# Moving the comparison of later choices into the loop over experts, and the choices of all four batches behind the end of L0

## The chip, the cores and the metric

The kernel runs on one core of a Trainium2 chip. Its time is the device time of one execution in microseconds (us), taken as the median of several runs. The engines are TensorE (PE for its matmuls, PEld for loading their stationary operand), VectorE (DVE), ScalarE (ACT), GpSimd (POOL) and SyncE (SP, which here only issues DMAs). Each works through its own instructions in their written order and waits for the others by semaphores.

## The reference

The program is two layers, L0 and L1, each an attention and a feed-forward part, over 4 batches of 256 tokens with 256 features, in float32. L0 is an attention with rounded weights and inputs, then a mixture of 32 experts; L1 is a cross attention and a gated feed-forward net. What matters here is L0's mixture of experts:

```python
router_probs = softmax(x @ gate_weight.T)
router_top_value, router_indices = top_k(router_probs, 8)
routing_weights = router_top_value / clip(sum(router_top_value), 1e-12)
prim, sec = router_indices[:, :4], router_indices[:, 4:]
sim_cand = sim[sec[:, :, None], prim[:, None, :]]
best_sim, best_i = max(sim_cand, -1), argmax(sim_cand, -1)
new_sec = where(best_sim < 0.5, sec, prim[best_i])
combine = sum(one_hot(concat(prim, new_sec)) * routing_weights)
y = sum over experts e of combine[:, e] * (silu(x @ wg[e].T) * (x @ wu[e].T)) @ wd[e].T
```

(x is the layer-normed input; the result is added to the residual stream. Lines are shortened.) Each token has eight chosen experts. The four later choices are compared with the four first ones by a table of similarities, and a later choice that is similar enough hands its weight to a first one. What is left with a weight of its own among the later choices is computed by a rarely needed second pass.

L1's attention lets a token see only the keys whose number lies in a window that ends at the token's segment id; the mask of that window is called `bad` in the kernel.

## The kernel before, in words

**L0's attention** runs as 16 units: four groups of heads (c) times four batches (b), unit u = 4c + b. Each unit is cut into small steps (projection, norms, scores, softmax, gather, rounding, output), and the order of all steps of all units is written out: `PLACE` gives each kind of step a place, `SHIFT` moves it by unit, and line 977 sorts them into one list, `line`. Each engine issues its steps in that order. A hundred places are meant as about one us. Step Y (line 887) adds a unit's output to the residual stream `xs`; the last, of unit 15, is the end of L0, and `done` is its place.

**The route of a batch** (class `Route`) is put into the same list when the last group of heads (units 12 to 15) is reached. Its steps: statistics and mean of the rows (DVE, lines 299 and 302), an epsilon, the power that makes the reciprocal deviation (POOL, line 308), the norm (DVE, 311), the turn by transposes (PE, 320) and its copy (ACT, 323), the router's logits (PE, 329), maximum, exponential and softmax (337 to 347), the choice of eight (351, 352), its one-hot form (357), the members of each expert (364), ranks within an expert by matmuls (PE, 374 to 381), places (389, 392) and goals (397 to 402). A step's place is that of the batch's own Y plus 100 times the step's number plus `WAIT` of the batch.

**The set-up of L1** folds weights of L1's attention (lines 1053 to 1129, mostly PE and ACT) and is placed from `done` on, spaced by `SPREAD`. All of this is under a hand-written order, up to line 1146.

**From line 1147 on a planner places the instructions**: it takes them in written order as priority, but may put one that is ready into a hole of its engine earlier. First come the 32 scatters (line 406: POOL issues a DMA that writes 128 rows of a batch to the rows `rows_in` of their experts in DRAM), eight a batch, then the slots (416, 417). Then comes the comparison: four transposes of the one-hots of later choices into a bank (1180), their copy (1184), a matmul with the similarities for each of eight row tiles (1189), a product (1191) and a sum (1197) on DVE, then a score of small DVE steps that end in the weights `wf` (1221) and the flag `isleft` (1227, 1229), and the mask `bad` (1239 to 1243).

**The loop over experts** (1308 to 1321) has 34 turns. In a turn it issues the load of an expert's 256 rows `xe` (SP, 1282), their transposes (PE, 1290) and the copy `xeT` (DVE, 1292), the gate and up products of the expert before (PE 1273, ACT 1275, DVE 1276), and the down product of the one before that (PE 1299, ACT 1304) with its write to `rows_out` (SP, 1305). The weights of two experts are loaded at a time. After the loop the flag is read (1323) and, if it is set, the second pass runs. Then L1's attention gathers rows back with POOL's DMAs (1355), weights them by `wf` (1358), and goes on to the rest.

Tiles live in pools. Those of the set-up lie in `set1`, as do those of the comparison; `set1` is closed before the loop's pool `experts` is opened, so that its tiles take the same memory.

Of the kernel before, what the change touches and what calls it, by code (L numbers as in the profile page):

```python
# [7 lines left out]
F32 = mybir.dt.float32  # L8
# [4 lines left out]
I32 = mybir.dt.int32  # L13
AF = mybir.ActivationFunctionType
ALU = mybir.AluOpType
AX = mybir.AxisListType
PSUM, DRAM = bass.MemoryType.PSUM, bass.MemoryType.DRAM

P = 128
B, S, H = 4, 256, 256  # L20
SC = 64
# [33 lines left out]

WAIT = [50, 52, 21, 0]
SPREAD = 135


PLACE = {
# [46 lines left out]
def build(tc, ctx, t, out):  # L109
# [7 lines left out]
    def bank(name):  # L117
        return psum.tile([P, 512], F32, tag="bank", name=name)
# [143 lines left out]
    class Route:  # L262
# [24 lines left out]

        def get(self, tag, shape, dtype=F32):
            if tag not in self.tile:
                self.tile[tag] = small.tile(shape, dtype, tag="rt_" + tag, bufs=2, name=f"rt_{tag}_{self.name}")  # L290
            return self.tile[tag]

        def bank(self, name):
# [125 lines left out]
        def parts(self):  # L419

            d = [
                (0.2, self.stats, 0), (0.6, self.stats, 1), (1.0, self.mean, 0), (1.2, self.mean, 1), (1.5, self.eps),
                (2.0, self.power), (3.2, self.norm, 0), (3.7, self.norm, 1), (4.8, self.turn), (6.0, self.turned),
                (7.5, self.logits), (9.0, self.largest), (9.8, self.exponential), (10.4, self.softmax),
                (11.2, self.choose, 0), (11.6, self.choose, 1), (12.2, self.choices), (13.2, self.members),
                (14.6, self.ranks), (15.8, self.places), (16.8, self.goals),
            ]
            return d

    routes = [Route(b) for b in range(B)]  # L430
    with ExitStack() as l0:
# [532 lines left out]
                d["Y"] = (0, self.residual)  # L964
                return d

        line = []
        for u in range(4 * B):
            for name, (kind, *call) in Unit(u).parts().items():
                place = PLACE[name] + SHIFT[0][u] + (SHIFT[kind][u] if kind else 0)  # L970
                line.append((place, u, name, call))
                if name == "Y":
                    done = place
            if u >= 3 * B:
                for m, (behind, *call) in enumerate(routes[u - 3 * B].parts()):
                    line.append((done + 100 * (behind + WAIT[u - 3 * B]), u, f"route{m:02d}", call))
        line.sort(key=lambda x: x[:3])

        later = [x for x in line if x[0] > done]
# [52 lines left out]
    with moe as l0:  # L1032
# [123 lines left out]

        one = set1.enter_context(tc.tile_pool(name="moe1", bufs=1, reuse_waits="tile"))
        work = set1.enter_context(tc.tile_pool(name="moe", bufs=1, reuse_waits="tile"))  # L1160
        offd = one.tile([P, P], F32, name="offd")
        nc.vector.tensor_scalar(offd[:], ident[:], -1.0, 1.0, ALU.mult, ALU.add)
        nc.vector.tensor_tensor(simb[:], simb[:], offd[:], ALU.mult)
        nc.vector.tensor_tensor(simb[:], simb[:], ident[:], ALU.add)
        ones = one.tile([P, P], F32, name="ones")
        nc.gpsimd.memset(ones[:], 1.0)

        wt = route.tile([P, NT, TOPK], F32, name="wt")
        m8 = one.tile([P, NT], F32, name="m8")
        nc.vector.tensor_reduce(m8[:], tv[:], AX.X, ALU.add)  # L1170
        nc.vector.tensor_scalar(m8[:], m8[:], 1e-12, None, ALU.max)
        nc.vector.reciprocal(m8[:], m8[:])
        nc.vector.tensor_tensor(wt[:], tv[:], m8[:].unsqueeze(2).to_broadcast([P, NT, TOPK]), ALU.mult)

        cand = one.tile([P, NT, NSEL, NSEL], F32, name="cand")
        for m in range(2):
            pt = bank(f"ps_oh_{m}")
            for i in range(4):
                n = 4 * m + i
                nc.tensor.transpose(  # L1180
                    pt[:, i * P : (i + 1) * P], routes[n // 2].oh()[:, n % 2, NSEL:, :].rearrange("p k e -> p (k e)"), ident[:]
                )
            ohT = work.tile([P, 512], F32, tag="ohT", name=f"ohT_{m}")
            nc.scalar.copy(ohT[:], pt[:])
            rows = bank(f"ps_sim_{m}")
            for i in range(4):
                n = 4 * m + i
                cut = slice(i * P, (i + 1) * P)
                nc.tensor.matmul(rows[:, cut], ohT[:, cut], simb[:], start=True, stop=True)
                pd = work.tile([P, NSEL, NSEL, NE], F32, tag="pd", name=f"pd_{n}")  # L1190
                nc.vector.tensor_tensor(
                    pd[:],
                    rows[:, cut].rearrange("p (j e) -> p j e", j=NSEL).unsqueeze(2).to_broadcast([P, NSEL, NSEL, NE]),
                    routes[n // 2].oh()[:, n % 2, :NSEL, :].unsqueeze(1).to_broadcast([P, NSEL, NSEL, NE]),
                    ALU.mult,
                )
                nc.vector.tensor_reduce(cand[:, n], pd[:], AX.X, ALU.add)

        cv = cand[:].rearrange("p n j i -> p (n j) i")
        NJ = NT * NSEL  # L1200
        best = one.tile([P, NJ], F32, name="best")
        nc.vector.tensor_reduce(best[:], cv, AX.X, ALU.max)
        eq = one.tile([P, NJ, NSEL], F32, name="eq")
        nc.vector.tensor_tensor(eq[:], cv, best[:].unsqueeze(2).to_broadcast([P, NJ, NSEL]), ALU.is_equal)
        left = one.tile([P, NJ], F32, name="left")
        nc.vector.tensor_scalar(left[:], eq[:, :, 0], -1.0, 1.0, ALU.mult, ALU.add)
        for i in range(1, NSEL):
            nc.vector.tensor_tensor(eq[:, :, i], eq[:, :, i], left[:], ALU.mult)
            if i < NSEL - 1:
                nc.vector.tensor_tensor(left[:], left[:], eq[:, :, i], ALU.subtract)  # L1210
        wu = one.tile([P, NJ], F32, name="wu")
        wuv = wu[:].rearrange("p (n j) -> p n j", n=NT)
        nc.vector.tensor_scalar(wu[:], best[:], THRESHOLD, None, ALU.is_ge)
        nc.vector.tensor_tensor(wuv, wuv, wt[:, :, NSEL:], ALU.mult)
        nc.vector.tensor_tensor(wt[:, :, NSEL:], wt[:, :, NSEL:], wuv, ALU.subtract)
        nc.vector.tensor_tensor(eq[:], eq[:], wu[:].unsqueeze(2).to_broadcast([P, NJ, NSEL]), ALU.mult)
        gain = one.tile([P, NT, NSEL], F32, name="gain")
        nc.vector.tensor_reduce(gain[:], eq[:].rearrange("p (n j) i -> p n i j", n=NT), AX.X, ALU.add)
        nc.vector.tensor_tensor(wt[:, :, :NSEL], wt[:, :, :NSEL], gain[:], ALU.add)

        nc.vector.tensor_tensor(wf[:], wt[:, :, :NSEL], room[:], ALU.mult)
        nc.vector.tensor_tensor(wt[:, :, :NSEL], wt[:, :, :NSEL], wf[:], ALU.subtract)
        some = one.tile([P, 1], F32, name="some")
        nc.vector.tensor_reduce(some[:], wt[:].rearrange("p n k -> p (n k)"), AX.X, ALU.max)
        nc.vector.tensor_scalar(some[:], some[:], 0.0, None, ALU.is_gt)
        ps = bank("ps_left")
        nc.tensor.matmul(ps[:, :1], ones[:], some[:], start=True, stop=True)
        isleft = route.tile([P, 1], I32, name="isleft")
        nc.vector.tensor_scalar(isleft[:], ps[:, :1], 0.0, None, ALU.is_gt)


        seg = one.tile([P, NT], F32, name="seg")
        nc.vector.tensor_copy(seg[:], segi[:])
        seglo = one.tile([P, NT], F32, name="seglo")
        nc.vector.tensor_scalar(seglo[:], seg[:], -float(LOOKBACK), None, ALU.add)
        kid = one.tile([P, SC], F32, name="kid")
        nc.gpsimd.iota(kid[:], [[1, SC]], base=0, channel_multiplier=0, allow_small_or_imprecise_dtypes=True)
        for n in range(NT):
            nc.vector.tensor_scalar(bad[:, n, :], kid[:], seg[:, n : n + 1], None, ALU.is_le)
            nc.vector.scalar_tensor_tensor(  # L1240
                bad[:, n, :], kid[:], seglo[:, n : n + 1], bad[:, n, :], ALU.is_ge, ALU.mult
            )
        nc.vector.tensor_scalar(bad[:], bad[:], -1.0, -NEG, ALU.add, ALU.mult)

        set1.close()
        ew = {}
        work = l0.enter_context(tc.tile_pool(name="experts", bufs=3, reuse_waits="tile"))
# [1 line left out]
        def expert_weights(g):  # L1249
# [11 lines left out]
            )  # L1261
            return w


        def products(w, j, x, width, name):

# [41 lines left out]
        for step in range(NE + 2):  # L1308
            if step < NE:
                if step % EW == 0:  # L1310
                    ew[step // EW] = expert_weights(step // EW)
                xe[step] = taken(step)
            if step == 6:
                nc.sync.dma_start(w_dq[:], t["W_dq"].rearrange("(k p) n -> p k n", p=P))
                nc.sync.dma_start(w_qr[:], t["W_qr"])
                nc.sync.dma_start(w_qrs[:], t["W_qrs"])
# [293 lines left out]
```

## Time and profile before

| what | us |
|---|---|
| median of 3 runs | 924.29 (923.53 to 925.32) |
| the profiled execution, its own time | 923.63 |
| its span, first to last instruction | 921.8 |
| last Y (end of L0) begins | 519.38 |
| scatters of batch 0 on POOL | 498.5 to 509.4 |
| scatters of batch 1 | 524.2 to 534.2 |
| scatters of batches 2 and 3 | 538.1 to 558.1 |
| first transposes of expert rows | 581.5 |
| first gather back | 690.3 |

Over the span PE is busy 84%, DVE 67%, ACT 46% and POOL 44%, and the mean granted clock of PE is 0.93 of full speed.

How to read a line of the engines in order of time: start in us, length in us, engine, line of the kernel, operation, output<-inputs, sizes, count; in brackets how long the engine sat idle before and what released it. A matmul of float32 shows as two instructions. "SPq" is SP issuing a DMA, where the length includes standing in its queue; several may be merged in one line. Places where L0 ends and the experts begin lie between 480 and 600 us.

### The profile page before, as it was taken

What the parts mean: (1) busy time and instruction counts of PE and PEld (TensorE: products, weight loads), DVE (VectorE), ACT (ScalarE), POOL (GpSimd) and SP (SyncE); (2) the same over time, 40 slices, a digit from 0 to 9 for tenths busy, and PEclk for the clock granted to TensorE, in tenths of its full rate; (3) what the DMA queues carried; (4) which work ended last, traced back from release to release, by engine and by line L of the source; (5) the groups of instructions that cost most, each with busy time, mean ns of one, the idle gap of its engine ahead of it and who ended that gap; (6) DMA issues with size and microseconds to landing.
All of it is one profiled execution on the core that took longest, in us unless ns stands there. A gap on an engine that the chain in (4) does not pass through costs nothing. (4 is left out here: it accounts for less than half of the span.)

```text
span 921.8 us, 12377 instructions
## 1 busy us (share of the span) xinstructions
PE 773.5 (84%) x4026; PEld 589.9 (64%) x4026; DVE 620.2 (67%) x1649; ACT 420.5 (46%) x1111; POOL 405.1 (44%) x442
## 2 busy tenths in 40 slices
PE   1687998999989989989896897799951778897996
PEld 1466776787767778777774663688840566675454
DVE  3989989788998788887886755433314786665211
ACT  1567785588766758567582243133320111212210
POOL 2556655456564754657556561000006773341001
PEclk8679999999999999999998897799985797999999
DMA  4201101002010100830009522488834210000001
GB/s 152 69 1 47 35 1 58 1 1 81 1 58 1 47 24 1 287 125 1 2 1 220 163 102 74 129 272 270 275 111 137 65 41 1 1 0 7 0 9 37
DMA packets 46101, 66.97 MB, mean 73 GB/s; under 512 B 6672, under 2 KB 28880, under 8 KB 45968
## 3 DMA queue, kind: packets, MB, share of 16 engines
q1 hardware_dynamic: 41872, 56.17, 19.8%
q0 software_dynamic: 3072, 8.39, 2.8%
q10 hardware_dynamic: 1088, 1.57, 0.5%
q8 instruction: 33, 0.54, 0.3%
q14 instruction: 36, 0.29, 0.1%
HBM read 44.10 MB, written 22.02 MB: 72 GB/s over the span
## 5 line engine op out<-in xcount | busy, mean ns | idle before, releaser
L578 POOL TENSOR_TENSOR hn_rs<-hn_var,mhalf 128x6 f32<-128x6 f32 (+1 forms) x64 | 76.5, 1211 | 90.0 <-DVE hn_var L571 82.0
L1355 POOL DMA_INDIRECT y<-rows_out,slot x32 | 32.2, 1005 | 146.9 <-issue 136.0
L560 POOL TENSOR_TENSOR fp_q<-cat,cc 128x1024 fp32r<-128x1024 bf16 x32 | 69.0, 2156 | 51.1 <-DVE cat L558 32.9
L782 POOL TENSOR_SCALAR p<-p,rc 128x256 f32<-128x256 f32 x128 | 65.6, 528 | 26.6 <-DVE rc L777 20.3
L727 ACT ACTIVATE qn_x<-ps_px,hn_nb,hn_rs 128x128 f32<-128x128 f32 x128 | 48.2, 457 | 50.0 <-DVE hn_nb L582 45.6
L880 PE MATMUL ps_y<-wp,fp_q 128*128 128x256 f32 x512 | 69.2, 293 | 2.0 <-issue 2.0
L880 PEld LDWEIGHTS ps_y<-wp,fp_q 128*128 128x128 f32 x512 | 64.4, 195 | 7.1 <-issue 6.8
L771 ACT ACTIVATE p<-ps_s,mx 128x256 f32<-128x256 f32 x128 | 62.2, 511 | 12.0 <-DVE mx L764 11.6
L800 PE MATMUL ps_o<-pT,v 128*128 128x512 f32 x128 | 64.5, 628 | 3.1 <-ACT pT L793 2.8
L753 PE MATMUL ps_s<-kT,qT 128*128 128x256 f32 x256 | 65.8, 386 | 0.6 <-ACT qn_q L727 0.5
L1273 PE MATMUL ps_g<-xeT,wgu 128*96 128x256 f32 x256 | 62.3, 387 | 0.0
L727 ACT ACTIVATE qn_q<-ps_pq,hn_nb,hn_rs 128x128 f32<-128x128 f32 x128 | 53.0, 481 | 1.7 <-DVE hn_nb L582 1.7
L753 PEld LDWEIGHTS ps_s<-kT,qT 128*128 128x128 f32 x256 | 45.4, 192 | 7.3 <-issue 1.8
L764 DVE TENSOR_REDUCE mx<-ps_s 128x2 f32<-128x512 f32 x64 | 43.3, 681 | 7.3 <-PE ps_s L753 6.9
L1273 PEld LDWEIGHTS ps_g<-xeT,wgu 128*96 128x96 f32 x256 | 40.9, 167 | 11.1 <-DVE xeT L1292 0.3
L582 DVE SCALAR_TENSOR_TENSOR hn_nb<-hn_ms,hn_rs 128x6 f32<-128x6 f32 (+1 forms) x64 | 34.0, 532 | 19.1 <-POOL hn_rs L578 16.6
L808 ACT ACTIVATE cat<-ps_o,r_sm 128x256 bf16<-128x256 f32 x64 | 27.5, 491 | 37.1 <-PE ps_o L800 37.1
L1276 DVE TENSOR_TENSOR hT<-hT,ps_g 96x256 f32<-96x256 f32 x32 | 13.3, 417 | 45.3 <-ACT hT L1275 45.3
L793 ACT COPY pT<-ps_pt 128x512 f32<-128x512 f32 x64 | 38.2, 630 | 10.0 <-PE ps_pt L789 10.0
L1275 ACT ACTIVATE hT<-ps_g 96x256 f32<-96x256 f32 x32 | 12.2, 380 | 63.5 <-PE ps_g L1273 63.5
L703 PE MATMUL ps_px<-wqx,xq 128*128 128x512 f32 x128 | 40.1, 436 | 0.6 <-DVE wqx L533 0.3
L789 PE MATMUL ps_pt<-ident,p 128*128 128x128 f32 x256 | 37.6, 274 | 3.2 <-POOL p L782 3.1
(290 smaller groups left out, 2041.6 us busy)
## 6 DMA issues: line engine op xcount, KB each, us to landing
rows_in<-zeros SPq DMA_DIRECT2D x4, 2048.0 KB, 16.1
xe<-rows_in SPq DMA_DIRECT2D x32, 256.0 KB, 3.9
rows_out<-ye SPq DMA_DIRECT2D x32, 256.0 KB, 3.5
wgu<-in_wgu SPq DMA_DIRECT2D x16, 384.0 KB, 4.0
wp<-in_wproj SPq DMA_DIRECT2D x8, 512.0 KB, 3.9
wd<-in_wd SPq DMA_DIRECT2D x16, 192.0 KB, 3.2
w_W_o<-in_W_o SPq DMA_DIRECT2D x1, 2048.0 KB, 9.8
wq<-in_wq SPq DMA_DIRECT2D x3, 512.0 KB, 4.3
```

What stands on the lines that cost most here:

```text
L560: nc.gpsimd.tensor_tensor(dst, y, cb, ALU.subtract)
L578: nc.gpsimd.tensor_tensor(rs[:, a:z], var[:, a:z], mhalf[:, a:z], ALU.pow)
L703: nc.tensor.matmul(dst, xq[self.b][:, j, k, tok], wt[:, k, half, :], start=(k == 0 and half == 0), stop=(k == KC - 1 and half == 1))
L727: nc.scalar.activation(qn[:, cut], src[:, cut], AF.Identity, bias=nb[:, at + h : at + h + 1], scale=rs[:, at + h : at + h + 1])
L753: nc.tensor.matmul(sc[:, h * S : (h + 1) * S], qT[:, 2 * g + h, i * P : (i + 1) * P], kT[:, g, :], start=True, stop=True)
L764: nc.vector.tensor_reduce(self.four("mx", g)[:, 2 * i : 2 * i + 2], self.bank(f"s_{g}{i}")[:].rearrange("p (h s) -> p h s", h=2), AX.X, AL ...
L771: nc.scalar.activation(self.p(g, i)[:, h, :], self.bank(f"s_{g}{i}")[:, h * S : (h + 1) * S], AF.Exp, bias=self.four("mx", g)[:, at], accu ...
L782: nc.gpsimd.tensor_scalar(p[:, h, :], p[:, h, :], self.four("rc", g)[:, at], 1.0, ALU.mult, ALU.mult)
L793: nc.scalar.copy(pT[:, :, :, i * P : (i + 1) * P], self.bank(f"pt_{g}{i}")[:].rearrange("p (m h s) -> p m h s", m=2, h=2))
L800: nc.tensor.matmul(o[:], v[:, m, g * D : (g + 1) * D], pT[:, m].rearrange("p h s -> p (h s)"), start=(m == 0), stop=(m == 1))
L880: nc.tensor.matmul(y[:, i * H : (i + 1) * H], q[:, h, i * P : (i + 1) * P], wp[self.c][:, 4 * j + h, m, :], start=(fresh and h == 0 and m ...
L1273: nc.tensor.matmul(dst, w["gu"][:, j, m, k, :], x[:, k], start=(k == 0), stop=(k == KC - 1))
```

## The change

It has three parts.

1. The routes of all four batches are placed by one clock: by `done`, the place of the last Y, instead of each by its own batch's Y. `WAIT` becomes -7, 0, 3, 6 (times 100 places) and a new `LAG` of 1.6 is added behind the power, and half of it again before the softmax. The small tiles of a route have four buffers instead of two.
2. `SPREAD` goes from 135 to 120, so that the set-up's steps are placed closer together.
3. The comparison, the flag and the mask become a function, `what_is_left`, with the same instructions in the same order. It is called in the loop over experts, at step 8, behind that step's `taken`; its tiles come from the loop's pool `experts` (one buffer each), and `set1` is closed before.

```diff
-WAIT = [50, 52, 21, 0]
-SPREAD = 135
+WAIT = [-7, 0, 3, 6]
+LAG = [1.6, 1.6, 1.6, 1.6]
+SPREAD = 120
...
-                self.tile[tag] = small.tile(shape, dtype, tag="rt_" + tag, bufs=2, name=f"rt_{tag}_{self.name}")
+                self.tile[tag] = small.tile(shape, dtype, tag="rt_" + tag, bufs=B, name=f"rt_{tag}_{self.name}")
...
-                (2.0, self.power), (3.2, self.norm, 0), (3.7, self.norm, 1), (4.8, self.turn), (6.0, self.turned),
-                (7.5, self.logits), (9.0, self.largest), (9.8, self.exponential), (10.4, self.softmax),
-                (11.2, self.choose, 0), (11.6, self.choose, 1), (12.2, self.choices), (13.2, self.members),
-                (14.6, self.ranks), (15.8, self.places), (16.8, self.goals),
+                (1.6, self.power), (1.6 + LAG[self.b], self.norm, 0), (2.1 + LAG[self.b], self.norm, 1), (3.2 + LAG[self.b], self.turn), (4.4 + LAG[self.b], self.turned),
+                (5.9 + LAG[self.b], self.logits), (7.4 + LAG[self.b], self.largest), (8.2 + LAG[self.b], self.exponential),
+                (8.8 + LAG[self.b] * 1.5, self.softmax), (9.6 + LAG[self.b] * 1.5, self.choose, 0), (10.0 + LAG[self.b] * 1.5, self.choose, 1),
+                (10.6 + LAG[self.b] * 1.5, self.choices), (11.6 + LAG[self.b] * 1.5, self.members),
+                (13.0 + LAG[self.b] * 1.5, self.ranks), (14.2 + LAG[self.b] * 1.5, self.places), (15.2 + LAG[self.b] * 1.5, self.goals),
...
-        line = []
+        line, chosen = [], []
...
-                    line.append((done + 100 * (behind + WAIT[u - 3 * B]), u, f"route{m:02d}", call))
+                    chosen.append((100 * (behind + WAIT[u - 3 * B]), u, f"route{m:02d}", call))
+        line += [(done + behind, *x) for behind, *x in chosen]
...
-        one = set1.enter_context(tc.tile_pool(name="moe1", bufs=1, reuse_waits="tile"))
-        work = set1.enter_context(tc.tile_pool(name="moe", bufs=1, reuse_waits="tile"))
-        offd = one.tile([P, P], F32, name="offd")
...
         set1.close()
         ew = {}
         work = l0.enter_context(tc.tile_pool(name="experts", bufs=3, reuse_waits="tile"))
...
+        def what_is_left():
+
+            offd = work.tile([P, P], F32, name="offd", bufs=1)
+            nc.vector.tensor_scalar(offd[:], ident[:], -1.0, 1.0, ALU.mult, ALU.add)
...
+            for m in range(2):
+                pt = bank(f"ps_oh_{m}")
...
+                ohT = work.tile([P, 512], F32, tag="ohT", bufs=1, name=f"ohT_{m}")
+                nc.scalar.copy(ohT[:], pt[:])
...
+                    pd = work.tile([P, NSEL, NSEL, NE], F32, tag="pd", bufs=1, name=f"pd_{n}")
...
+            nc.vector.tensor_scalar(bad[:], bad[:], -1.0, -NEG, ALU.add, ALU.mult)
+            return wt, isleft
...
                 xe[step] = taken(step)
+            if step == 8:
+                wt, isleft = what_is_left()
             if step == 6:
```

More of the change, by code (lines that the diff above doesn't have):

```diff
@@ L1152, in build @@
             r.slots()
-        one = set1.enter_context(tc.tile_pool(name="moe1", bufs=1, reuse_waits="tile"))
-        work = set1.enter_context(tc.tile_pool(name="moe", bufs=1, reuse_waits="tile"))
-        offd = one.tile([P, P], F32, name="offd")
[L1162 to L1243, printed above, removed]
         set1.close()
@@ L1262, in expert_weights @@
             return w
+        def what_is_left():
+            offd = work.tile([P, P], F32, name="offd", bufs=1)
+            nc.vector.tensor_scalar(offd[:], ident[:], -1.0, 1.0, ALU.mult, ALU.add)
+            nc.vector.tensor_tensor(simb[:], simb[:], offd[:], ALU.mult)
+            nc.vector.tensor_tensor(simb[:], simb[:], ident[:], ALU.add)
+            ones = work.tile([P, P], F32, name="ones", bufs=1)
+            nc.gpsimd.memset(ones[:], 1.0)
+            wt = route.tile([P, NT, TOPK], F32, name="wt")
+            m8 = work.tile([P, NT], F32, name="m8", bufs=1)
+            nc.vector.tensor_reduce(m8[:], tv[:], AX.X, ALU.add)
+            nc.vector.tensor_scalar(m8[:], m8[:], 1e-12, None, ALU.max)
+            nc.vector.reciprocal(m8[:], m8[:])
+            nc.vector.tensor_tensor(wt[:], tv[:], m8[:].unsqueeze(2).to_broadcast([P, NT, TOPK]), ALU.mult)
+            cand = work.tile([P, NT, NSEL, NSEL], F32, name="cand", bufs=1)
+            for m in range(2):
+                pt = bank(f"ps_oh_{m}")
+                for i in range(4):
+                    n = 4 * m + i
+                    nc.tensor.transpose(
+                        pt[:, i * P : (i + 1) * P], routes[n // 2].oh()[:, n % 2, NSEL:, :].rearrange("p k e -> p (k e)"), ident[:]
+                    )
+                ohT = work.tile([P, 512], F32, tag="ohT", bufs=1, name=f"ohT_{m}")
+                nc.scalar.copy(ohT[:], pt[:])
+                rows = bank(f"ps_sim_{m}")
+                for i in range(4):
+                    n = 4 * m + i
+                    cut = slice(i * P, (i + 1) * P)
+                    nc.tensor.matmul(rows[:, cut], ohT[:, cut], simb[:], start=True, stop=True)
+                    pd = work.tile([P, NSEL, NSEL, NE], F32, tag="pd", bufs=1, name=f"pd_{n}")
+                    nc.vector.tensor_tensor(
+                        pd[:],
+                        rows[:, cut].rearrange("p (j e) -> p j e", j=NSEL).unsqueeze(2).to_broadcast([P, NSEL, NSEL, NE]),
+                        routes[n // 2].oh()[:, n % 2, :NSEL, :].unsqueeze(1).to_broadcast([P, NSEL, NSEL, NE]),
+                        ALU.mult,
+                    )
+                    nc.vector.tensor_reduce(cand[:, n], pd[:], AX.X, ALU.add)
+            cv = cand[:].rearrange("p n j i -> p (n j) i")
+            NJ = NT * NSEL
+            best = work.tile([P, NJ], F32, name="best", bufs=1)
+            nc.vector.tensor_reduce(best[:], cv, AX.X, ALU.max)
+            eq = work.tile([P, NJ, NSEL], F32, name="eq", bufs=1)
+            nc.vector.tensor_tensor(eq[:], cv, best[:].unsqueeze(2).to_broadcast([P, NJ, NSEL]), ALU.is_equal)
+            left = work.tile([P, NJ], F32, name="left", bufs=1)
+            nc.vector.tensor_scalar(left[:], eq[:, :, 0], -1.0, 1.0, ALU.mult, ALU.add)
+            for i in range(1, NSEL):
+                nc.vector.tensor_tensor(eq[:, :, i], eq[:, :, i], left[:], ALU.mult)
+                if i < NSEL - 1:
+                    nc.vector.tensor_tensor(left[:], left[:], eq[:, :, i], ALU.subtract)
+            wu = work.tile([P, NJ], F32, name="wu", bufs=1)
+            wuv = wu[:].rearrange("p (n j) -> p n j", n=NT)
+            nc.vector.tensor_scalar(wu[:], best[:], THRESHOLD, None, ALU.is_ge)
+            nc.vector.tensor_tensor(wuv, wuv, wt[:, :, NSEL:], ALU.mult)
+            nc.vector.tensor_tensor(wt[:, :, NSEL:], wt[:, :, NSEL:], wuv, ALU.subtract)
+            nc.vector.tensor_tensor(eq[:], eq[:], wu[:].unsqueeze(2).to_broadcast([P, NJ, NSEL]), ALU.mult)
+            gain = work.tile([P, NT, NSEL], F32, name="gain", bufs=1)
+            nc.vector.tensor_reduce(gain[:], eq[:].rearrange("p (n j) i -> p n i j", n=NT), AX.X, ALU.add)
+            nc.vector.tensor_tensor(wt[:, :, :NSEL], wt[:, :, :NSEL], gain[:], ALU.add)
+            nc.vector.tensor_tensor(wf[:], wt[:, :, :NSEL], room[:], ALU.mult)
+            nc.vector.tensor_tensor(wt[:, :, :NSEL], wt[:, :, :NSEL], wf[:], ALU.subtract)
+            some = work.tile([P, 1], F32, name="some", bufs=1)
+            nc.vector.tensor_reduce(some[:], wt[:].rearrange("p n k -> p (n k)"), AX.X, ALU.max)
+            nc.vector.tensor_scalar(some[:], some[:], 0.0, None, ALU.is_gt)
+            ps = bank("ps_left")
+            nc.tensor.matmul(ps[:, :1], ones[:], some[:], start=True, stop=True)
+            isleft = route.tile([P, 1], I32, name="isleft")
+            nc.vector.tensor_scalar(isleft[:], ps[:, :1], 0.0, None, ALU.is_gt)
+            seg = work.tile([P, NT], F32, name="seg", bufs=1)
+            nc.vector.tensor_copy(seg[:], segi[:])
+            seglo = work.tile([P, NT], F32, name="seglo", bufs=1)
+            nc.vector.tensor_scalar(seglo[:], seg[:], -float(LOOKBACK), None, ALU.add)
+            kid = work.tile([P, SC], F32, name="kid", bufs=1)
+            nc.gpsimd.iota(kid[:], [[1, SC]], base=0, channel_multiplier=0, allow_small_or_imprecise_dtypes=True)
+            for n in range(NT):
+                nc.vector.tensor_scalar(bad[:, n, :], kid[:], seg[:, n : n + 1], None, ALU.is_le)
+                nc.vector.scalar_tensor_tensor(
+                    bad[:, n, :], kid[:], seglo[:, n : n + 1], bad[:, n, :], ALU.is_ge, ALU.mult
+                )
+            nc.vector.tensor_scalar(bad[:], bad[:], -1.0, -NEG, ALU.add, ALU.mult)
+            return wt, isleft
```

## The prediction

> **What bounds the kernel now.** I read the row of granted clock on the page first, then a table of stretches around the end of L0, then each engine in order of time from 480 to 600 us, and last the loads of `xe`. Stretches (start:end, length, busy us of PE, PEld, DVE, ACT, POOL with counts, clock, DMA share, GB/s):
>
> ```profile
> 480.00:500.00 20.00, 16.60 (x98) 12.18 (x97) 17.26 (x48) 9.78 (x27) 10.21 (x11) 0.91 0.80 178
> 500.00:519.40 19.40, 11.00 (x56) 8.76 (x57) 12.12 (x36) 1.68 (x4) 12.14 (x12) 0.74 0.31 95
> 519.40:563.00 43.60, 42.00 (x177) 26.69 (x176) 18.70 (x96) 22.36 (x43) 25.67 (x28) 1.00 0.51 165
> 563.00:581.50 18.50, 7.12 (x26) 4.68 (x26) 16.10 (x38) 2.46 (x3) 0.00 (x0) 0.60 0.04 16
> 600.00:650.00 50.00, 50.00 (x264) 40.84 (x263) 18.19 (x33) 15.48 (x33) 0.00 (x0) 1.00 0.87 271
> ```
>
> The set-up of L1 (row 3) and the experts (row 5) are PE's. Two stretches are not: the end of L0 (row 2: PE 11.0 of 19.4) and the comparison (row 4: DVE 16.1 of 18.5, PE nearly idle). Why, from the engines in order of time:
>
> ```profile
> 494.15 0.16 DVE L777 RECIPROCAL rc<-sm 128x4 f32<-128x4 f32 x1
> 494.51 2.36 POOL L782 TENSOR_SCALAR p<-p,rc 128x256 f32<-128x256 f32 x4 [1.27 <-DVE tif L355]
> 506.36 0.96 POOL L406 DMA_INDIRECT rows_in<-kept,goal  x1 [0.30 <-issue]
> 507.34 0.73 POOL L308 TENSOR_TENSOR rt_rs<-rt_ve,mhalf 128x2 f32<-128x2 f32 x1
> 508.11 0.47 DVE L311 TENSOR_SCALAR kept<-xs,rt_mv,rt_rs 128x256 f32<-128x256 f32 x1 [6.54 <-POOL rt_rs L308]
> 508.73 0.66 PE L320 MATMUL ps_m<-ident,kept 128*128 128x128 f32 x2 [6.92 <-DVE kept L311]
> 519.38 0.74 DVE L887 SCALAR_TENSOR_TENSOR xs<-ps_y,pscale,xs 128x512 f32<-128x512 f32 x1
> ```
>
> Batch 0's scatters sit on POOL ahead of batch 1's power (L308). DVE stands 6.54 us for that power, and the last unit's rounding, queued behind it on DVE, stands too. Earlier, the last unit's reciprocal, whose inputs ACT finished at 484.3, is issued only at 494.15, behind batch 0's choices.
>
> ```profile
> 538.11 0.96 POOL L406 DMA_INDIRECT rows_in<-kept,goal  x1 [3.90 <-DVE goal L402]
> 557.18 0.96 POOL L406 DMA_INDIRECT rows_in<-kept,goal  x1 [0.30 <-issue]
> 559.59 28.37 SPq L1282 DMA_DIRECT2D xe<-rows_in  x7
> 562.82 0.66 PE L1180 MATMUL ps_oh<-ident,kept 128*128 128x128 f32 x4
> 581.50 1.95 PE L1290 MATMUL ps_xe<-ident,xe 128*128 128x128 f32 x8
> ```
>
> The first experts' rows are asked for at 559.6 (landing is 3.9 us in the median), but PE turns to them at 581.5, behind the comparison. So the end follows: end of L0, set-up, comparison, experts at 3.03 us each, gathers. From 581.5 on I take all lengths as unchanged and move only that start.
>
> **Step 1, the end of L0 moves earlier.** Let T be the last addition (L887), now 519.38. With the routes behind it, I redo the chain of units 14 and 15. Unit 14's L558 (0.68) goes at 483.5, where batch 0's stats stood; POOL's L560 (2.15) ends at 486.35. Its other half needs L552, L848, L554, L556, L558 (0.41+0.68+0.43+0.43+0.68=2.6) on DVE; I let these wait for L560, since L554 took 1.74 beside one: 489.0, then L560 to 491.1 (was 493.24). Four L782 follow to 493.0 (were 496.87), meanwhile PE does 16 of L880 to 493.3. Transposes, copies and L800 took 498.01 to 501.80, so they end at 497.1. Then ACT's L808 0.84, DVE's four steps 1.95, L560 2.13, L880 x16 2.5: T = 504.5. I add 1 us for a clock below 1.00 on some of it: **T = 505.5**. Bounds: PE's busy time from 483 to T without the routes is 17.3 (14.6+9.0 less 6.3 in L320, L329, L374 to L381), so not below 500.5; if only the 6.54 stall goes, 512.9.
>
> **Step 2, choices and scatters come later.** Batch 0's stats now follow the last unit's rounding, its turn (L320) the last L880. PE paces the rest, because set-up stands between: turn 0.75, L1057 1.1, logits 1.3, five key pairs and two folds at about 1.0 (7.0), batch 1's turn and logits 1.9, batch 2's turn 0.75: ranks at T+12.8. Then DVE finishes what is placed ahead (batch 1's maximum, batch 3's norm, 1.3), places 0.85 and goals 1.1: the first scatter at **T+16.3**, 521.8. All 32 now stand in one line (8 were done by 509.4 before): 31 x 1.266 + 0.96 = 40.2, the cadence being 538.11 to 557.18 over 15 steps. They end at 562.0, against 558.1. The other batches are placed 3, 7 and 10 us behind on a 17 us course; a batch of scatters takes 10.1, so they keep ahead. Here a rule speaks against the change. The Trainium skill, SBUF — State Buffer, "SBUF: two separate sides": while DVE runs a copy-like instruction in its two-port mode, GpSimd can't write the descriptors of its DMAs; a 620 ns DMA is given there as 3100 ns. The row: batch 1's eight scatters ran from 524.24 to 534.2, beside 5.2 us of DVE work, at the same 1.266 as batch 3's, beside none. By the rule, if half of the 24 scatters beside routes or comparison took 2.5 us more, 30 us; by the row, 0. I take the row, which is this very work.
>
> **Step 3, the experts start.** From the last scatter's end to the first load's issue is 559.59-558.14=1.45, landing 3.9: first transposes at 562.0+5.4+0.1 = **567.5** (T+62), 14.0 earlier than 581.5. Set-up ends before that: 518.7 to 562.9 is 44.2, plus 3.7 for batch 0's logits and ranks and batch 1's turn and logits that it newly holds, so T+48.5=554.0, leaving 13.5 us of slack. This slack hides SPREAD 135 to 120, the PE waits that denser work may bring, and the late load of `W_o`: released by the last L880, 9.8 us to land, first used by L1094 21.7 us behind T now. If set-up exceeds T+62, each us more costs one. Four buffers instead of two for the routes' small tiles cost nothing but a few bytes, and let four routes be open.
>
> **Step 4, the comparison in the loop.** The work itself is unchanged: DVE 11.0 (L1191, L1197, 16 x 0.69), about 4.5 in small steps, masks 4.5 (538.7 to 543.2); ACT 2 x 0.59; POOL 0.4; no DMA, so it passes nothing on SP's queue. On PE: eight transposes at 0.11 start to start, and sixteen half-matmuls at 0.11, half of L1273's 0.215: 2.6. Its results are late readers' only: the flag is read at L1323 (686), `wf` at 697, the mask at 715. What is queued behind its DVE instructions are L1276 and L1292, and PE waits for both one step on. DVE's spare is 3.03-0.42-0.69=1.9 us a step. Where the planner puts it isn't visible. Below: nothing, if it fills the 13.5 us between set-up and experts. Above: 16, if it stands as one block at step 8 (20 us of DVE less the spare of two steps). The nearest rows are the planner's own: masks, `ones` and `kid`, written after the set-up, ran at 518 to 543 in holes, the `W_dq` load of step 6 at 523.6. Tiles lying where set-up's lie must wait for these, so I take the hole from 554: 13.5 of the 18.6 us (562.8 to 581.4) fit, 5 us of DVE spill into the spare of three steps, 1 to 2 us of PE with it: **+1.5**.
>
> **Sum.** 923.63 - 14.0 + 1.5 = 911.1 for an execution like the profiled one (span 921.8, 1.8 around it). It lies 0.66 below the runs' median: 911.8, I say **912**.
>
> **Rivals.**
> (a) Comparison in the way, 0.20: wholly ahead of the experts in PE's order, first transposes at 554.0+18.6=572.6, 5 later: 917; as a tight block in the loop nearer its upper end, 922. For: priority may favour it at step 8, one buffer for `pd` and `ohT`. Against: the planner's hole-filling.
> (b) L0's end gives back only the stall, 0.10: T=512.9, 7.4 later: 919. For: cold clock of 0.50 to 0.70 in 509 to 517 may recur. Against: the reciprocal's ten idle us are removed too.
> (c) Slower, 0.14: the scatters become the bound. Place: POOL, behind the last goals. Batches 2 and 3 now start together, 18.7 behind T, with two routes on DVE; two more at about 7.7 each (rows L299 to L417 of batch 0) make 34.1. If the four finish nearly together like that, the first scatter starts at 539.6 and everything shifts by 17.8: 930. It decides from a first scatter at 521.8+12.5=534.3. For: PE and DVE serve four routes and the set-up at once. Against: batch 0 is placed 7 us ahead of the next one.
> (d) No change, 0.04, and slower for small mixed delays, 0.02: gains of 14 eaten by (a)'s block, 924 to 927.
>
> **How the numbers follow.** The likeliest case has 0.50, at 912, own range 906 to 916 (T from 501 to 508, comparison 0 to 4). With (a) and (b) faster has 0.80. A difference under 0.2% (1.8 us) can't be told from none: same 0.04, slower 0.16. Range 905 to 923: it takes in (a) and (b) and leaves out (c), and little below.
>
> **What will show it.** Right: no L406 before L887's last; L887's last at 501 to 509; DVE's 6.54 wait gone; 32 scatters in one line from about 522; first L1290 at 565 to 570; L1189 before or among the first steps, and steps of 3.03 elsewhere. Wrong: a first L406 past 534, a cadence over 1.3 beside DVE work, PE waiting for L1276 over several us about step 8, or a start of L1290 still behind the flag's matmul (L1227).

## The result: 0.3% slower, and the profile after

| | before | changed |
|---|---|---|
| median of 8 runs each, us | 924.09 (922.87 to 925.50) | 926.59 (925.39 to 928.53) |
| ratio to before | | 1.0028, 95% interval 1.0017 to 1.0040 |
| span of the profiled execution | 921.8 | 925.0 |
| end of L0 (last Y begins) | 519.38 | 505.52 |
| first expert transposes | 581.5 | 564.25 |
| first gather back | 690.34 | 693.65 |

The forecast was 912, faster. The table already says where it broke: the experts start 17.25 us earlier, and yet the first gather comes 3.3 us later. Lines of the changed kernel are two to some twenty higher than before: Y is L889, the scatter L407, the load of rows L1285, their transposes L1293, products L1276, the comparison's transposes, matmuls, product and flag L1202, L1211, L1213 and L1249.

The table of stretches for the changed kernel (start:end, length, busy us of PE, PEld, DVE, ACT, POOL with counts, clock, DMA share, GB/s), with its rows put at the new ends:

```profile
500.00:505.50 5.50, 3.39 (x28) 3.19 (x28) 4.11 (x9) 0.00 (x0) 3.30 (x3) 1.00 0.49 136
505.50:551.50 46.00, 45.13 (x208) 29.71 (x206) 26.31 (x122) 23.77 (x48) 26.96 (x29) 1.00 0.45 141
551.50:564.20 12.70, 0.00 (x0) 0.00 (x0) 1.60 (x4) 0.84 (x1) 7.08 (x9) 0.55 0.36 121
588.60:607.30 18.70, 6.97 (x29) 4.67 (x27) 15.28 (x35) 1.59 (x3) 0.00 (x0) 0.64 0.19 65
```

The end of L0 is short now and set-up is still PE's. Row 3 is the 12.7 us between set-up and the first rows: PE does nothing in it. Row 4 is the comparison at step 8, and it looks like row 4 of before moved 26 us to the right: 18.7 us, DVE 15.3 busy, PE 7.0, a low clock.

The same in the engines' order of time (start, length, engine, line, operation, in brackets the idle time before it and its releaser):

```profile
505.52 0.75 DVE L889 SCALAR_TENSOR_TENSOR xs<-ps_y,pscale,xs 128x512 f32<-128x512 f32 x1 [0.52 <-PE ps_y L882]
519.50 1.25 POOL L407 DMA_INDIRECT rows_in<-kept,goal  x1 [2.93 <-DVE to L417]
559.09 0.96 POOL L407 DMA_INDIRECT rows_in<-kept,goal  x1 [0.30 <-issue]
561.50 5.04 SPq L1285 DMA_DIRECT2D xe<-rows_in  x6
564.25 1.94 PE L1293 MATMUL ps_xe<-ident,xe 128*128 128x128 f32 x8 [12.78 <-DMA xe<-rows_in]
566.95 0.23 DVE L1185 TENSOR_SCALAR offd<-ident 128x128 f32<-128x128 f32 x1
588.62 0.60 PE L1202 MATMUL ps_oh<-ident,kept 128*128 128x128 f32 x4
591.17 0.49 PE L1211 MATMUL ps_sim<-simb,ohT 128*128 128x128 f32 x2 [0.35 <-DVE pd L1213]
600.47 0.80 PE L1211 MATMUL ps_sim<-simb,ohT 128*128 128x128 f32 x2 [0.78 <-DVE pd L1213]
606.84 0.56 PE L1249 MATMUL ps_left<-some,ones 128*128 128x1 f32 x2 [5.57 <-DVE some L1247]
607.26 3.71 PE L1276 MATMUL ps_g<-xeT,wgu 128*96 128x256 f32 x8
612.14 1.89 PE L1276 MATMUL ps_g<-xeT,wgu 128*96 128x256 f32 x8
```

The first five lines are the forecast's picture. From 588.62 PE is in the comparison: it makes a row tile's matmuls, waits for DVE to take them, and at the end waits 5.57 us for DVE's small steps before the flag's matmul. The next expert's products come behind the flag in PE's order, so they start only at 607.26, 18.64 after the place where they would have stood, and then take 3.71 for 1.89, at a granted clock of 0.50. DVE's L1185 is the exception: it is an instruction of the comparison, written at step 8, and the planner issued it at 566.95, beside the first expert.

### The profile page after: what moved, and what is told of

Read it like the earlier page. It is cut to its first block, busy times and chain, and to the rows that moved or that the text cites. A ratio compares the mean times of both kernels' runs of the same rounds, so it can differ in the third digit from the quotient of the medians.

```text
span 925.0 us, 12373 instructions
## 1 busy us (share of the span) xinstructions
PE 772.4 (84%) x4026; PEld 589.6 (64%) x4026; DVE 617.9 (67%) x1649; ACT 419.8 (45%) x1111; POOL 404.3 (44%) x442
## 5 line engine op out<-in xcount | busy, mean ns | idle before, releaser
L562 POOL TENSOR_TENSOR fp_q<-cat,cc 128x1024 fp32r<-128x1024 bf16 x32 | 68.9, 2154 | 56.6 <-DVE cat L560 37.2
L1276 PE MATMUL ps_g<-xeT,wgu 128*96 128x256 f32 x256 | 64.1, 396 | 0.0
L1276 PEld LDWEIGHTS ps_g<-xeT,wgu 128*96 128x96 f32 x256 | 41.8, 170 | 11.7 <-issue 0.4
L1279 DVE TENSOR_TENSOR hT<-hT,ps_g 96x256 f32<-96x256 f32 x32 | 13.3, 417 | 45.9 <-ACT hT L1278 45.9
L705 PE MATMUL ps_px<-wqx,xq 128*128 128x512 f32 x128 | 40.1, 436 | 0.6 <-DVE wqx L535 0.4
L1295 DVE COPY xeT<-ps_xe 128x512 f32<-128x512 f32 x32 | 22.1, 692 | 27.1 <-PE ps_xe L1293 27.1
```

The costliest lines, as they stand in the source:

```text
L562: nc.gpsimd.tensor_tensor(dst, y, cb, ALU.subtract)
L705: nc.tensor.matmul(dst, xq[self.b][:, j, k, tok], wt[:, k, half, :], start=(k == 0 and half == 0), stop=(k == KC - 1 and half == 1))
L1276: nc.tensor.matmul(dst, w["gu"][:, j, m, k, :], x[:, k], start=(k == 0), stop=(k == KC - 1))
```

## The experiments

**My theory after the result (1):** the placing part does what was forecast; the comparison in the loop costs its whole chain, since it stands as one block in PE's order, and the planner can't break it up, because PE's work takes banks of PSUM (the memory that matmuls write to) from one common ring of eight (`bank()`), handed out in written order. **Rivals:** the placing part gains nothing that lasts; only the two parts together hurt; the comparison costs the same spread out.

### Four kernels, on a chip where the kernel before itself took 931

Each part of the change alone, and two versions that keep the whole change but cut the comparison up. places_only is the kernel before with the first two parts of the change (places, buffers, `SPREAD`) and the comparison ahead of the loop as it was. compare_only is the changed kernel with these parts undone:

```diff
-WAIT = [-7, 0, 3, 6]
-LAG = [1.6, 1.6, 1.6, 1.6]
-SPREAD = 120
+WAIT = [50, 52, 21, 0]
+SPREAD = 135
...
-        line += [(done + behind, *x) for behind, *x in chosen]
```

In split and tile_a_step `what_is_left` is a generator that yields between its parts, and each row tile's product gets a bank of its own. split issues all but the flag's matmul and the mask ahead of the loop (first block below), tile_a_step one part in a step (second block):

```diff
-                rows = bank(f"ps_sim_{m}")
+                    rows = bank(f"ps_sim_{n}")
...
+        parts = what_is_left()
+        for _ in range(12):
+            next(parts)
...
+            if step >= 2:
+                next(parts, None)
```

> Only the new places of the routes, SPREAD and the four buffers; the comparison stays ahead of the experts, as before. Theory 1 (the placing gains, the comparison as a block in the loop loses it again): L0 ends at 505.5 as in the changed kernel, the comparison's 18.6 us follow the set-up's end at 551.5, first expert transposes at about 570 to 571 instead of 581.5: 11 us faster than before, 913. Theory 2 (the denser placing or the single line of 32 scatters costs what it gains): 924 or more.

> Only the comparison, flag and mask moved into the loop at step 8; places, SPREAD and buffers as before. Theory 1: first expert transposes at about 563.5, when their rows land (18 us earlier), then a block of 18.6 us at step 8 in which PE does nothing for the experts and 1.8 more for products at half clock: 18 won, 20.4 lost, 926.5. The prediction's view (the comparison fills holes, +1.5): 907.6.

> The changed kernel, but the transposes, similarities, products, sums and small steps are written ahead of the loop, each of the eight row tiles with a bank of its own, and only the flag's matmul and the mask at step 8. Theory 1: the eight tiles take about 12 us from 551.5, in which PE waits for the scatters anyway; first expert transposes at 564 to 565, no block in the loop: 20 us less than the changed kernel, 906 to 908. Theory 2 (the loss is elsewhere: masks on DVE in the loop, memory of the pools, the gathers): 920 or more.

> The changed kernel, but the comparison is cut into parts and one part is written in each step of the loop from step 2 on (four transposes and a copy, then one row tile a step with a bank of its own, later the small steps, the flag, the mask). Theory 1: only PE's own work is added, 2.6 us, DVE's 1.4 us a step fits the spare 1.9: 909 to 911. If any DVE work in the loop delays PE one for one, 16 us of it: 922.

Measured, beside 931.19 for the kernel before: places_only 930.43 (ratio 0.9994, 0.9981 to 1.0007), compare_only 933.95 (1.0023, 1.0007 to 1.0039), split 924.01 (0.9897, 0.9846 to 0.9947), tile_a_step 922.49 (0.9883, 0.9834 to 0.9932). compare_only met its expectation in the difference to before, 2.8 us for 2.5, but in part by luck: its experts began at 573.16, not at 563.5. The cut-up versions beat the kernel before, but by about half of what was expected (7.2 and 8.7 us, for 16 to 18 and 13 to 15), and places_only gained nothing. The blocks were as expected (split's flag matmul held PE for 0.3 us at step 8), and L0 ended at 508.1 in places_only and split. What differed lay in between, on ScalarE in split:

```profile
547.82 2.06 ACT L1111 COPY vo<-ps_vo 128x512 f32<-128x512 f32 x4
569.04 0.59 ACT L1101 COPY l1uvo<-ps_uvo 128x512 f32<-128x512 f32 x1 [19.16 <-remote]
```

"remote" is a release by nothing that this trace holds. Set-up stood 19 us for one copy in split and in tile_a_step, 8.1 in compare_only; in places_only VectorE stood 27.2 (L1121) and ScalarE three times for 2.2 to 2.9. In all four the last such wait ended 3.9 to 5.0 us after the last scatter began. In the changed kernel the copy in that place waited 2.56 us, for PE. So this set couldn't say what the placing is worth: either the new places bring such stretches about (theory B below; but compare_only has one without them), or the place where these ran does (theory A).

### The same, beside the kernels before and after

The copies are unchanged. own_bank is the changed kernel with one PSUM bank set apart for the comparison:

```diff
-    psum = ctx.enter_context(tc.tile_pool(name="psum", bufs=8, space=PSUM))
+    psum = ctx.enter_context(tc.tile_pool(name="psum", bufs=7, space=PSUM))
+    own = ctx.enter_context(tc.tile_pool(name="own", bufs=1, space=PSUM))
...
-                pt = bank(f"ps_oh_{m}")
+                pt = own_bank(f"ps_oh_{m}")
...
-                rows = bank(f"ps_sim_{m}")
+                rows = own_bank(f"ps_sim_{m}")
...
-            ps = bank("ps_left")
+            ps = own_bank("ps_left")
```

> The kernel before, unchanged, for a trace taken beside the others of this set. Theory A (the stretch in which ScalarE or VectorE stands still with no releaser that the trace shows, seen in the first set while the scatters run, belongs to the place of the run, the chip or its memory, not to the change): this trace shows such a stretch too, between its first scatter (about 538) and its last (about 578), or its span is 921 to 925 where the other three show none either. Theory B (the stretch belongs to the new placing of the choices): none here, while after_again and places_again show one.

> The changed kernel, unchanged, beside places_again and own_bank. Theory 1 (the comparison is one block at step 8 of the loop and costs 18.7 us of PE's order and 1.8 of a cold clock): 0.2 to 0.4% slower than before, the block again 18 to 19 us long. Theory A adds: if ScalarE stands still in set-up here, the span grows by what the stall pushes the first expert transposes behind 564.25. Theory B: it stands still here and not in the kernel before.

> Placing part alone, again. Undisturbed, the recorded steps give T at 505.5, last scatter at about 559, first expert transposes at the later of rows (564 to 567.5) and of the comparison ahead of the loop, which begins when set-up ends (551.5) and takes the 24 us it took before (557 to 581): 567 to 576, so 5 to 14 us faster than before. Theory A: where the trace shows no stretch without releaser, 0.6 to 1.5% faster; where it shows one of 8 to 27 us, within 0.3% as in the first set. Theory B: the stretch is here again wherever it is run, and the time is that of before.

> The changed kernel with one of its eight PSUM banks given to the comparison alone; nothing else is altered. Theory 1 with its cause (work that takes a bank of the common ring can't be issued past work written earlier; with a ring of its own it can): PE's order shows the comparison's 28 instructions spread over several steps, no idle PE over 2 us between 590 and 610, and the time is 12 to 18 us under the changed kernel's, less what seven banks cost the rest (0 to 6): 8 to 18 us under it. Rival (the planner leaves the comparison together whatever the banks): a block of 18 to 19 us remains and the time is that of the changed kernel or a little above.

Measured, beside 923.70 for the kernel before: after_again 927.64 (1.0041, 1.0029 to 1.0053), places_again 914.07 (0.9898, 0.9867 to 0.9929), own_bank 927.32 (1.0035, 1.0024 to 1.0047). after_again is at the upper end of its expectation, its block 18.6 us long; places_again met its own. No trace of this set has a "remote" wait on PE, DVE or ACT. That leaves theory B without ground, since places_again runs with the new places and has none, and it settles the first rival: **the placing part alone makes the kernel 1.0% faster.** Whether the kernel before shows such a stretch on the chip where it took 931 was not traced.

In places_again the comparison is the same chain in the old position, ahead of the experts:

```profile
556.35 0.66 PE L1183 MATMUL ps_oh<-ident,kept 128*128 128x128 f32 x4
574.92 0.56 PE L1230 MATMUL ps_left<-some,ones 128*128 128x1 f32 x2 [5.57 <-DVE some L1228]
575.34 1.95 PE L1293 MATMUL ps_xe<-ident,xe 128*128 128x128 f32 x8
```

It takes 19.0 us from its first transpose to the experts, as it took 18.7 in the kernel before. The rows were there some 6 of these us earlier: after_again's experts began 5.2 us behind its last scatter (561.01, 566.22), and here the last scatter is at 563.93. The other 12.8 lie in the gap between set-up and rows.

own_bank's time is that of the changed kernel, 8 to 18 us short of what theory 1 expected and what its rival forecast. Its trace says otherwise about the cause. PE around step 8, and the comparison's first transpose:

```profile
525.07 0.33 PE L1207 MATMUL ps_oh<-ident,kept 128*128 128x128 f32 x1 [2.43 <-DVE kept L363]
...
588.68 0.38 PE L1216 MATMUL ps_sim<-simb,ohT 128*128 128x128 f32 x2
588.90 1.03 PE L1307 MATMUL ps_y<-wd,hT 96*128 96x256 f32 x4
...
605.36 0.39 PE L1216 MATMUL ps_sim<-simb,ohT 128*128 128x128 f32 x2
605.58 1.46 PE L1281 MATMUL ps_g<-xeT,wgu 128*96 128x256 f32 x6
606.90 0.49 PE L1216 MATMUL ps_sim<-simb,ohT 128*128 128x128 f32 x2
...
625.48 0.35 PE L1254 MATMUL ps_left<-some,ones 128*128 128x1 f32 x2 [0.23 <-DVE some L1252]
```

The block is gone: the planner took the first transpose to 525 and strewed the row tiles' matmuls among the steps of the loop, and PE waits 0.23 us for the flag. But L0 now ended at 517.71, ten us later than in after_again. Whether that is the price of leaving the common ring only seven banks had to be measured by itself.

### The control, and the cut-up versions again

seven_banks is the changed kernel with `bufs=7` in the common ring and nothing else.

> Part of the comparison ahead of the loop (transposes, products and small steps, 7.4 us of PE's order in the first set, in the gap of 12.8 us that PE spends waiting for the first rows), the flag product and the mask in step 8. Theory 1: with no stretch of ScalarE without releaser, first expert transposes stay at the rows' 564 to 567, step 8 costs 0.3 us, so 17 to 20 us under the changed kernel and 1.6 to 2.0% under the one before. Rival (the loop with the placing part can't gain more than places_again showed, since the gap is filled by the comparison): about 1.0% under before, first expert transposes near 575.

> The comparison cut into parts, one to a step of the loop from step 2 on. Theory 1: no block, each step with a part 0.2 us longer (3.25 for 3.03 in the first set) plus the flag's wait of 1.5, so 15 to 18 us under the changed kernel, 1.3 to 1.8% under before, a little above split_again. Rival (each part in the loop pulls PE's clock or ScalarE's copies back): steps of 4 us or more, under 1.0% gained.

> The comparison in the loop alone, with the choices placed as before. Theory 1: it takes the 18.6 us ahead of the loop away (first expert transposes at set-up's end or the rows, about 566 to 568 in place of 584) and puts 20 in at step 8: 0.1 to 0.4% slower than before. Rival (the two parts of the change only hurt together): within 0.1% of before or faster.

> The changed kernel with seven PSUM banks in the common ring and the eighth unused: what own_bank pays for its bank. Theory 1: the end of L0 moves back as in own_bank (517.7 for 507.5, so 10 us), the block at step 8 stays 18 to 19 us, and the time is 8 to 13 us over the changed kernel's (own_bank's was level with it). Rival (own_bank's spread comparison itself costs what the block did): the time is own_bank's, within 0.3%.

Measured, beside 924.41: split_again 907.40 (0.9810, 0.9778 to 0.9841), tile_again 910.11 (0.9841, 0.9824 to 0.9859), compare_again 928.66 (1.0042, 1.0027 to 1.0058), seven_banks 940.10 (1.0154, 1.0137 to 1.0171). split_again and tile_again fell within theory 1's numbers, compare_again at its upper end, and seven_banks lost 12 to 14 us against the changed kernel's 926.6 and 927.6, at or just over its own. Its block at step 8 is there again, 18.7 us long:

```profile
602.69 0.60 PE L1202 MATMUL ps_oh<-ident,kept 128*128 128x128 f32 x4
620.97 0.56 PE L1249 MATMUL ps_left<-some,ones 128*128 128x1 f32 x2 [5.57 <-DVE some L1247]
621.38 3.71 PE L1276 MATMUL ps_g<-xeT,wgu 128*96 128x256 f32 x8
```

The traces of the result and of the last two sets in one table, each span cut at the same three events (us; first to last column: end of L0, from there to the first scatter, to the first expert transposes, from those to the first gather, and the time of the first gather):

| kernel | end of L0 = T | first scatter, T+ | first transposes, T+ | loop, to first gather | first gather |
|---|---|---|---|---|---|
| before | 519.38 | (batches apart) | 62.12 | 108.84 | 690.34 |
| before_again | 521.85 | (batches apart) | 62.15 | 108.46 | 692.46 |
| changed | 505.52 | 13.98 | 58.73 | 129.40 | 693.65 |
| after_again | 507.46 | 13.99 | 58.76 | 130.07 | 696.29 |
| places_again | 508.61 | 15.04 | 66.73 | 108.11 | 683.45 |
| compare_again | 523.38 | (batches apart) | 43.55 | 129.56 | 696.49 |
| seven_banks | 520.78 | 13.99 | 58.77 | 129.45 | 709.00 |
| own_bank | 517.71 | 18.20 | 62.96 | 112.19 | 692.86 |
| tile_again | 504.43 | 13.99 | 58.76 | 113.83 | 677.02 |
| split_again | 506.58 | 14.96 | 59.89 | 108.30 | 674.77 |

The column of the loop is the verdict. Every kernel with the comparison as a block at step 8 has 129.4 to 130.1, with whatever placing and with seven or eight banks. Every one with the comparison ahead of the loop has 108.1 to 108.8. So the block costs 20.6 us of the loop (129.40 less 108.84): 18.64 of chain, 1.82 by the half clock in the products behind it, and 0.1 more, nearly all of it in the down products that follow (1.11 for 1.03). own_bank against seven_banks differs in one thing, whose ring the comparison draws from, and falls from 129.45 to 112.19: 17.3 us for letting it pass. Its bank costs most of that again, at the end of L0 (T at 517.7 and 520.8, for 505.5 to 507.5) and in scatters that begin 4.2 us later behind it, so that own_bank's time shows nothing of the gain beside the changed kernel; beside seven_banks it is 12.8 us shorter.

split_again is the best of all here. PE in its gap and at step 8:

```profile
553.44 0.66 PE L1203 MATMUL ps_oh<-ident,kept 128*128 128x128 f32 x4
563.51 0.80 PE L1213 MATMUL ps_sim<-simb,ohT 128*128 128x128 f32 x2 [2.61 <-DVE pd L1215]
566.47 1.94 PE L1298 MATMUL ps_xe<-ident,xe 128*128 128x128 f32 x8 [2.16 <-DMA xe<-rows_in]
589.80 0.28 PE L1253 MATMUL ps_left<-some,ones 128*128 128x1 f32 x2
589.94 1.95 PE L1281 MATMUL ps_g<-xeT,wgu 128*96 128x256 f32 x8
```

Its transposes and matmuls run from 553.4 to 564.3, and the experts still wait 2.16 us for their rows: the gap hides the part of the chain that PE takes part in. The small DVE steps run beside the first experts, and the flag's matmul, eight steps later, has nothing to wait for. tile_again pays instead 3.25 us for each of its steps with a part (tiles at 572.92, 576.18, 579.43) against 3.03, waits 1.45 us for the flag, and begins on a colder clock (first products 3.70 for 2.76): 113.83, 5.5 more than split_again. This answers the other two rivals: compare_again is slower without the new places, and the comparison spread out costs 5.0 us of the loop (113.83 less 108.84), not 20.6.

## Why the prediction was wrong

**Step 1 held.** T was forecast at 505.5 and measured at 505.52; PE's granted clock is 1.00 in the stretch before it, where before it was 0.74. That the last us is right is luck: 1 us was added for a clock below 1.00, and was used up by DVE instead, about 0.5 by the end of POOL's second L560 (L562 now, 491.66 for 491.1) and 0.6 in its last four steps (2.5 for 1.95). The second trace has 507.46. The bound of 17.3 us for PE should be 18.3, since PE is busy 24.6 us from 483 to T, not 23.6.

**Step 2 held, 2.3 us early.** First scatter 521.8 forecast, 519.50 measured (T+13.98 for T+16.3; the terms written there add to 16.05); all 32 in one line. The cadence stayed: 31 gaps in 39.59 us, 1.277 mean, although DVE was 8 to 9 us busy in each ten of 515 to 535. So the 30 us estimated there from the rule of the Trainium skill (SBUF — State Buffer, "SBUF: two separate sides"), that two-port DVE work holds up descriptor writing, are not in this trace either. Which of this DVE work runs in that mode no trace tells, so the rule itself is not tested.

**Step 3 held, 3.3 us early.** First transposes 567.5 forecast, 564.25 measured, since the scatters ended 1.9 us earlier and PE began 2.75 us after the first load was issued rather than 3.9. Set-up ended at 551.5 for 554.0, with a gap of 12.7 for 13.5 (its own terms, 562.9 and 3.7 less T's 13.9, make 552.7). `W_o` landed in 8.6 us and L1097 waited for nothing.

**Step 4 failed.** It put the comparison in the loop at +1.5, because the nearest rows "ran at 518 to 543 in holes", with 16 as its upper bound. It measured +20.6 (129.40 less 108.84). Two things were wrong in it.

The first is the row that I took as nearest. Masks, `ones` and `kid` are DVE and POOL work that needs no PSUM bank, and they behaved as the row said, here too: `offd` went from step 8 to 566.95. The comparison's chain begins with transposes into a bank. own_bank against seven_banks shows that the ring is what kept it in place. The right row stood in the profile of before, in the prediction's own fence: the first rows were asked for at 559.59 and needed 3 to 4 us, and yet PE, 7.12 us busy in the 18.5 from 563.0, left their transposes until the flag was done. A planner that could pass bank-taking work could have filled that hole; that the ring is the reason there too is inferred, no run tested it in that place.

The second is the price. I counted the block as DVE's 20 us less two steps' spare, 16. But PE stands behind the flag for the chain's whole length, waits and all (18.64, the 18.6 that I had read off before), then starts on a cold clock (1.8). DVE's spare is no help to an engine that waits in order. So the upper bound was low by 4.6.

**Sum:** -17.25 + 20.56 = +3.31 to the first gather, and the spans differ by 3.2 (925.0 less 921.8).

**The rivals.** (a) had the mechanism, "a tight block in the loop", for 917 to 922; with the true price it is a loss, which I gave 0.02 in (d), "gains of 14 eaten by (a)'s block, 924 to 927". Its other half, the comparison wholly ahead of the experts at a price of 5 against the forecast, is what places_again ran: 9.6 us faster than before, where that half meant 7. (b) and (c) did not come about: the L0 end gave all of 13.9, and the first scatter came 15 us before the point from which (c) decides. Of the signs of being right, "L1189 before or among the first steps" failed: that matmul (L1211 now) first ran at 589.90, at step 8. Of the signs of being wrong none came as written. The nearest is "PE waiting for L1276 over several us about step 8": PE did stand there, but in front of the flag's matmul, 5.57 us for DVE's small steps (L1247), not for the experts' own product (L1276, now L1279).

## What to carry to other kernels

Before you price a moved piece of work at "a hole will take it", look whether an instruction that takes the same kind of buffer, and was ready, ever passed it in the trace; work on another engine with no such buffer is no evidence. Price a serial chain at its length from the first to the last instruction on the engine that has to wait in order, not at its busy time less somebody's spare. And where a chain must go somewhere, cut it: the part that holds the waiting engine into a gap that is there anyway (here 12.7 us before the first rows), the rest beside other work, and what reads the result late; with the placing, itself 1.0%, that was worth 1.9% here, where the whole change with the move in one block lost 0.3%.

## What the runs showed that I had not expected

- After the block PE's eight products took 3.71 us for 1.89, once, and the next ones 1.89 again: the granted clock was 0.50 from 607.26 to 610.76 and 1.00 from 612.14 on. So 18.7 us with PE 7.0 busy were enough to lose the clock, and one expert's products to regain it.
- One PSUM bank fewer moved the end of L0 by 13 to 15 us (520.78 for 505.52 and 507.46) and made the kernel 12 to 14 us slower. PE's waits fit that: its query projection (L705) waited 7.4 us, in four waits, for DVE's copy `pxT` out of another bank, a tile that the projection doesn't read; in the changed kernel it waited 0.7 us, once. The profile of before already has such a row, 2.9 us of PE's L734 for DVE's maximum `mx` (L764).
- The "remote" stretches of the first set, 8 to 27 us on ScalarE or VectorE during the scatters, came in four of four traces where the kernel before took 931 us, and in none of the ten where it took 924, with the same four kernels among both. In split, tile_a_step and compare_only it was the same instruction, the fourth copy of `l1uvo`. What held it is open: no run here tells an instruction that arrived late from another cause.
